# Key norms of an l2-normalised attention: spread over the key columns through DRAM, or transposed on TensorE and read by the exponentials as scales

## The chip, the core and the metric

The kernel runs on one core of one Trainium2 chip. A core has five engines, each with its own in-order instruction queue: TensorE (PE in the profile; its weight loads are listed as PEld), VectorE (DVE), ScalarE (ACT), GpSimd (POOL) and SyncE (SP, which here only starts DMAs). They work on a scratchpad of 128 partitions (SBUF) and on eight accumulator banks (PSUM, 2 KB per partition each), and wait for each other through semaphores.

The metric is the device time of one execution in microseconds (us), lower is better. Before the change three runs took 1624.97, 1627.02 and 1626.72 us, median 1626.72. The profile comes from one further execution.

## The reference, cut to what matters

The input is 8 sequences (batches) of 512 rows of 256 numbers. A layer of attention with 16 heads of 64 and a feed-forward part of four layers of width 1024 follow each other, each between two layer norms and with a residual.

```python
q = (x @ w_q).reshape(b, s, h, -1).transpose(0, 2, 1, 3)
...
q = _l2norm(q) * jnp.exp(scale)      # t / max(norm(t), 1e-12), per row and head
k = _l2norm(k)
sim = jnp.einsum('bhid,bhjd->bhij', q, k)
attn = jax.nn.softmax(sim, axis=-1)
out = jnp.einsum('bhij,bhjd->bhid', attn, v)
out = out.transpose(0, 2, 1, 3).reshape(b, s, h * out.shape[-1])
return out @ w_out + b_out
```

A score is the product of a query and a key, divided by the norm of each. The division by the key's norm can stand before the product, on the key, or behind it, on the score: it is one factor per key and head.

## The kernel before

**Where things lie.** The attention is computed transposed. For a batch and a half of the heads (8 heads, `hf` is 0 or 1) `qT` and `kT` hold four tiles of 128 x 512: the partitions are the 64 dimensions of two heads, the columns the 512 positions. A unit is a batch and a pair of heads (64 units). `scores` multiplies, for one block `jb` of 128 key positions, each head's keys with its queries: the result `s` has the 128 keys on the partitions and 2 x 512 columns, one bank for each head. One exponential over all 1024 columns (L555) gives `e`, without the subtraction of a maximum, since scores are bounded. `values` multiplies `e` with the values into `po`; `summed` adds the four blocks' `e` on DVE, and `row_sums` sums over the keys on PE for the softmax's denominator.

**The norms before.** `norms_step(b, hf, which)` runs for `which` "q" and "k". The squares (L427) are summed over each head's dimensions by four matmuls with a constant of ones and zeros (`pn`, L456), which leave each head's 512 sums on 16 equal partitions. ACT copies them to SBUF (`nd`, L480). A DMA takes one row of each head and folds the 8 x 512 numbers into 128 x 32 (`nf`, L462), DVE puts a floor under them (L488), POOL raises them to the power -1/2 (L312). For queries only, DVE multiplies by the head's exponentiated scale (L495). A DMA stores them to DRAM (L502), two more read them back, each head's row repeated over its 64 partitions (`spread`, L470), and four multiplications on DVE (L512) bring `qT` or `kT` to unit length. So a norm's way goes PE, ACT, DMA, DVE, POOL, DMA, DMA, DVE, and the scores of the half wait at its end.

**What sets the order.** All work of the attention is handed to `Steps`: each step names its engine, an estimated length, what it reads, writes and which rotating buffers it takes. PE's steps keep the order in which they are added; the other engines' steps are sorted by a small simulation in which of those that are ready the one with the earliest due time goes first. The order so found is fixed in the program. A loop over the units adds the scores of the next unit, the values of the present one, and from a `plan` by slots (two slots a unit, 16 a batch) the projections, norms, output projections and layer norms of neighbouring batches. In the first batch all projections come ahead of the units. In later ones the first half of a batch is prepared in the second part of the batch before it (keys' norm products at slot 9, values at 9 and 11 to 13), the second half in the batch's own first slots (norm products at slot 2, values at 3, 5, 6 and 7, among the previous batch's output projections at 2 to 5). DVE and SP have a second task in the first 300 us: all feed-forward weights are loaded (L854), looked through (L861, L866), combined and stored (L898, L902).

**Buffers that matter here.** The pool `ps_w` has three PSUM buffers, taken in turn by all projections, norm products, row transposes and row sums; a taker waits until the buffer of the third before it has been read. `ps_s` has two buffers of two banks for `s`, so the scores of a block wait for the exponential two blocks earlier. `sqp` has two SBUF buffers, for `nd` and the copied row sums. `ep` has six for `e`, `spreadp` two for the squares and the spread norms.

Of the kernel before, what the change touches and what calls it, by code (L numbers as in the profile page):

```python
# [12 lines left out]
AF = mybir.ActivationFunctionType  # L13
ALU = mybir.AluOpType
# [3 lines left out]
P = 128  # L18
LN_EPS = 1e-5
NORM_FLOOR = 1e-12  # L20
# [119 lines left out]
def tile_fast(  # L140
# [41 lines left out]
    nc = tc.nc  # L182

    B, S, D = x.shape
# [4 lines left out]
    NT = S // P  # L189
# [5 lines left out]
    HH = H // 2  # L195
# [4 lines left out]
    small = ctx.enter_context(tc.tile_pool(name="small", bufs=4))  # L200
# [8 lines left out]
    ident = const.tile([P, P], F32, name="ident")  # L209
# [16 lines left out]
    xres, T = {}, {}  # L226
# [14 lines left out]
    escale = const.tile([P, 2], F32, name="escale")  # L241
# [31 lines left out]
    for name, src in (("s1", s1), ("s2", s2), ("hs1", hs1), ("hs2", hs2)):  # L273
        t = const.tile([P, NH], F32, tag=name, name=f"{name}_sb")
# [7 lines left out]
    ep = attn_scope.enter_context(tc.tile_pool(name="ep", bufs=6))  # L282
# [4 lines left out]
    ps_w = attn_scope.enter_context(tc.tile_pool(name="ps_w", bufs=3, space=PSUM))  # L287
# [4 lines left out]
    steps = Steps()  # L292
# [6 lines left out]
    def bounded():  # L299

        nc.vector.tensor_reduce(top, escale, AX.X, ALU.max)
        nc.vector.tensor_scalar(over, top, SCORE_BOUND, None, ALU.is_gt)
        nc.vector.tensor_scalar_min(escale, escale, SCORE_BOUND)
# [3 lines left out]
        writes=[("escale", 0)], earliest=landed["escale"],  # L307
# [3 lines left out]
    def power(d, n):  # L311
        nc.gpsimd.tensor_tensor(d, d, neghalf.to_broadcast([P, n]), ALU.pow)  # L312

    def tile_of(pool, shape, tag, key, dtype=F32, bufs=None):
        T[key] = pool.tile(shape, dtype, tag=tag, bufs=bufs, name="_".join(str(k) for k in key))
        return T[key]
# [127 lines left out]

    def norms_step(b, hf, which):

        n = (which, b, hf)
        pn, d, f, r = ("pn", *n), ("nd", *n), ("nf", *n), ("spread", *n)
        to = (which + "T", b, hf)
        r_dram = dram.tile([HH, S], F32, tag=f"n{which}_{b}_{hf}", name=f"n{which}_{b}_{hf}")  # L450
        NF = HH * S // P

        def products():
            tile_of(ps_w, [P, S], "w", pn)
            for j in range(HP):
                nc.tensor.matmul(  # L456
                    T[pn][ts(j, 32), :], lhsT=halves_of, rhs=T[r][:, j, :], start=True, stop=True
                )

        def folded():  # L460
            tile_of(small, [P, NF], "nf", f, bufs=2)
            nc.sync.dma_start(  # L462
                T[f],
                T[d][::16, :].rearrange("i (c n) -> i c n", c=16),
            )

        def spread():
            tile_of(spreadp, [P, HP, S], "spread", r)
            for h in range(2):
                nc.sync.dma_start(  # L470
                    T[r][ts(h, DH)],
                    r_dram.rearrange("(j h) s -> h j s", h=2)[h : h + 1].to_broadcast([DH, HP, S]),
                )

        steps.add(
            "pe", 0.86, products, reads=[(r, j) for j in range(HP)], writes=[(pn, 0)],
            takes=[("w", 3, pn)], tiling=("col", 32),
        )
        steps.add(
            "act", 0.59, lambda: nc.scalar.copy(tile_of(sqp, [P, S], "sq", d), T[pn]),  # L480
            reads=[(pn, 0)], writes=[(d, 0)], takes=[("sq", 2, d)],
        )
        steps.add(
            "sync", 0.1, folded, reads=[(d, 0)], writes=[(f, 0)], takes=[("nf", 2, f)], lag=1.8
        )
        steps.add(
            "dve", 0.12,
            lambda: nc.vector.tensor_scalar_max(T[f], T[f], NORM_FLOOR * NORM_FLOOR),  # L488
            writes=[(f, 0)],
        )  # L490
        steps.add("pool", 6.0, lambda: power(T[f], NF), writes=[(f, 0)])
        if which == "q":
            steps.add(
                "dve", 0.12,
                lambda: nc.vector.tensor_scalar(  # L495
                    T[f], T[f], escale[:, hf : hf + 1], None, ALU.mult
                ),
                reads=[("escale", 0)], writes=[(f, 0)],
            )
        steps.add(  # L500
            "sync", 0.1,
            lambda: nc.sync.dma_start(r_dram.rearrange("i (c n) -> (i c) n", c=16), T[f]),  # L502
            reads=[(f, 0)], writes=[(("rd", *n), 0)], lag=1.5,
        )
        steps.add(
            "sync", 0.2, spread, reads=[(("rd", *n), 0)], writes=[(r, j) for j in range(HP)],
            lag=7.5,
        )
        for j in range(HP):
            steps.add(  # L510
                "dve", 0.69,
                lambda j=j: nc.vector.tensor_tensor(  # L512
                    T[to][:, j, :], T[to][:, j, :], T[r][:, j, :], ALU.mult
                ),
                reads=[(r, j)], writes=[(to, j)],
            )

    def v_step(b, hf, t):
        pm, to = ("vp", b, hf, t), ("v", b, hf)
        projected(pm, b, t, wkv_sb, INNER + hf * HALF)  # L520

        def copied():
            if t == 0:
                tile_of(vp, [P, NT, HALF], "v", to)
            nc.scalar.copy(T[to][:, t, :], T[pm])

        steps.add(
            "act", 0.59, copied, reads=[(pm, 0)], writes=[(to, t)],
            takes=[("v", 2, to)] if t == 0 else (),
        )  # L530

    def scores(b, p, jb):

        hf, j = divmod(p, HP)
        qT, kT, s, e = ("qT", b, hf), ("kT", b, hf), ("s", b, p, jb), ("e", b, p, jb)

        def products():
            tile_of(ps_s, [P, 2, S], "s", s)
            for h in range(2):
                hp = slice(h * DH, (h + 1) * DH)  # L540
                nc.tensor.matmul(  # L541
                    T[s][:, h, :],
                    lhsT=T[kT][hp, j, ts(jb, P)],
                    rhs=T[qT][hp, j, :],
                    start=True,
                    stop=True,
                )

        steps.add(
            "pe", 0.86, products, reads=[(kT, j), (qT, j)],  # L550
            writes=[(s, 0)], takes=[("s", 2, s)], tiling="row",
        )
        steps.add(
            "act", 1.03,
            lambda: nc.scalar.activation(tile_of(ep, [P, 2, S], "e", e), T[s], AF.Exp),  # L555
            reads=[(s, 0)], writes=[(e, 0)], takes=[("e", 6, e)],
        )

    def summed(b, p, jb):
# [208 lines left out]
    def at(slot, step):  # L768
        plan.setdefault(slot, []).append(step)
# [11 lines left out]
    def v_plan(b, hf, slots):  # L781
        for t, s in enumerate(slots):
            at(s, lambda t=t: v_step(b, hf, t))

    def next_rows(b, slot, some):
        if b < B:
            for t in some:
                at(slot + t // 2, lambda t=t: norm_in(b, "a", t, ("xres", b)))

    for b in range(B):  # L790
        base = b * NSLOT
        next_rows(b + 1, base, (0, 2))
        if b:
            qk_plan(b, 1, [base + s for s in (-2, -2, -1, -1, 0, 0, 1, 1)], (base, base + 2))
        next_rows(b + 1, base, (1, 3))
        if b:
            v_plan(b, 1, [base + s for s in (3, 5, 6, 7)])
            for t in range(NT):
                at(base + 2 + t, lambda b=b, t=t: out_proj(b - 1, t))
            n = b - 1 + NX  # L800
            if n < B:
                at(base + 6, lambda n=n: loads(n))
            elif n < B + 2:
                at(base + 6, lambda c=n - B: reloads(c))
        if b + 1 < B:
            qk_plan(
                b + 1, 0, [base + s for s in (6, 6, 7, 7, 8, 8, 9, 9)], (base + 8, base + 9),
                lambda b=b: v_step(b + 1, 0, 0),
            )
            for t in range(1, NT):  # L810
                at(base + 10 + t, lambda b=b, t=t: v_step(b + 1, 0, t))

    def loads(b):
        steps.add(
            "sync", 0.1, lambda: load_x(b), lag=4.0, writes=[(("xres", b), t) for t in range(NT)],
            takes=[("xres", NX, ("xres", b))],
        )
# [128 lines left out]
    for t in range(NT):  # L946
        v_step(0, 0, t)
        if t == 0:
            norms_step(0, 0, "k")
    for w in "qk":  # L950
        for j in range(HP):
            qk_step(0, 1, w, j)
    norms_step(0, 1, "q")
    for t in range(NT):
        v_step(0, 1, t)
    norms_step(0, 1, "k")
    units = [(b, p) for b in range(B) for p in range(NP)]
    for g in range(2):
        for jb in (2 * g, 2 * g + 1):
# [1 line left out]
    for k, u in enumerate(units):  # L961
# [3 lines left out]
        for g in range(2):  # L965
# [3 lines left out]
            if g == 0:  # L969
# [5 lines left out]
                b, p = u  # L975
# [16 lines left out]
    for t in range(NT):  # L992
# [6 lines left out]
        reads=[(("e", *units[-1], NT - 1), 0)],  # L999
# [36 lines left out]
    before, steps = steps, Steps()  # L1036
# [966 lines left out]
```

## Time and profile before

| | us |
|---|---|
| Median of three runs | 1626.72 |
| The profiled execution, whole | 1627.83 |
| Its span, first to last instruction | 1626.0 |
| Attention, up to the feed-forward part's first matmul | about 1022 |
| Steady batch (start of its first scores to that of the next, 397.60 to 523.05) | 125.4 |
| PE, DVE, ACT, POOL busy in 300 to 426 | 125.8, 57.3, 65.3, 27.2 |

The page shows busy time by engine, the busy share of 40 equal slices of the span, DMA queues, the chain of work that ended last, and groups of instructions: line, engine, operation, output and inputs, shapes, count, then busy time, mean ns of one, and the engine's idle time before them with what ended it. The timeline lists instructions in order of time with start and length, equal ones merged; in brackets stands the idle time before them and its releaser. The clock column is TensorE's granted clock as a share of full speed.

```profile
PE   9999999999999999999999999999999999999997
DVE  3587886454354363363363375869786987879686
ACT  4665445545545535635535634466566646654663
POOL 4211303302212122122112120447155426534451
PEclk9999999999999999999999999999999999999999
DMA  6446555222133122122122131444414532452440
```

PE's row is at nine tenths or more from end to end. The groups of the key chain that are on DVE, POOL and ACT:

```profile
L512 DVE TENSOR_TENSOR kT<-kT,spread_k 128x512 f32<-128x512 f32 x64 | 41.7, 685 | 18.3 <-DMA spread_k<-nk 13.2 <-ACT spread_k L427 5.1
...
L480 ACT COPY nd_k<-pn_k 128x512 f32<-128x512 f32 x16 | 9.4, 585 | 4.4 <-PE pn_k L456 3.9 <-DVE mv_a L332 0.5
...
L488 DVE TENSOR_SCALAR nf_k<-nf_k 128x32 f32<-128x32 f32 x16 | 2.8, 178 | 22.1 <-DMA nf_k<-nd_k 22.1
```

### The profile page before, as it was taken

The page shows a single profiled execution, that of the slowest core. Times are in us where ns is not written, and L with a number is a line of the kernel's source. Part 1 is how long each engine was busy: PE and PEld are TensorE (multiplying, and loading weights), DVE is VectorE, ACT ScalarE, POOL GpSimd, SP SyncE. Part 2 cuts the span into 40 slices and gives each one's busy share as a digit, 9 for nine tenths or more (in the row PEclk, how much of TensorE's full clock was granted, in tenths as well). Part 3 has the DMA queues.
Part 4 walks back from the last instruction along what each step waited for, and adds up shares of the span by engine and source line. Part 5 has one row for each costly group of instructions (what it writes and reads, how often), then busy time and mean ns, then how long its engine had stood idle before and what let it go on. Part 6 is the DMA issues. An engine that isn't in the chain of part 4 may idle for free.

```text
span 1626.0 us, 18855 instructions
## 1 busy us (share of the span) xinstructions
PE 1603.5 (99%) x6808; PEld 915.9 (56%) x6808; DVE 1023.9 (63%) x1708; ACT 878.2 (54%) x1343; POOL 487.5 (30%) x356
## 2 busy tenths in 40 slices
PE   9999999999999999999999999999999999999997
PEld 4333443443443443353353354788888888888886
DVE  3587886454354363363363375869786987879686
ACT  4665445545545535635535634466566646654663
POOL 4211303302212122122112120447155426534451
PEclk9999999999999999999999999999999999999999
DMA  6446555222133122122122131444414532452440
GB/s 177 119 139 169 151 181 132 68 66 67 41 79 67 42 79 67 41 74 63 43 75 66 29 92 27 143 129 132 147 61 143 156 113 79 141 157 66 132 154 29
DMA packets 91042, 159.91 MB, mean 98 GB/s; under 512 B 23868, under 2 KB 39484, under 8 KB 86844
## 3 DMA queue, kind: packets, MB, share of 16 engines
q1 hardware_dynamic: 71324, 95.71, 22.3%
q0 software_dynamic: 18912, 61.87, 12.3%
q8 instruction: 55, 0.90, 0.2%
q10 hardware_dynamic: 704, 1.05, 0.2%
q14 instruction: 47, 0.39, 0.1%
HBM read 140.26 MB, written 17.56 MB: 97 GB/s over the span
## 4 chain that ended last, share of the span: by engine, by line
PE 82%; DVE 3%; issue 2%; DMA 2%; POOL 1%; ACT 1%; SPq 0%; DVEq 0%; POOLq 0%
PE g L1256 25%; PE s L541 12%; PE po L586 11%; PE p L1182 6%; PE pa L711 6%; PE kp L411 5%; PE qp L411 5%; PE vp L387 5%; PE py L1370 3%; PE pd L609 2%; DMA spread_k<-nk 1%; POOL nf_k L312 1%; DMA nk<-nf_k 1%; PE pn_q L456 1%; PE pn_k L456 1%
## 5 line engine op out<-in xcount | busy, mean ns | idle before, releaser
L555 ACT ACTIVATE e<-s 128x1024 f32<-128x1024 f32 x256 | 248.2, 1021 | 120.8 <-PE s L541 120.3
L541 PE MATMUL s<-qT,kT 64*128 64x512 f32 x1024 | 255.8, 618 | 6.2 <-DVE kT L512 4.7
L586 PE MATMUL po<-e,v 128*64 128x512 f32 x1024 | 234.4, 600 | 0.0
L1256 PE MATMUL g<-h,wb_S 128*128 128x512 f32 x1024 | 234.3, 389 | 0.0
L312 POOL TENSOR_TENSOR nf_q<-nf_q,neghalf 128x32 f32<-128x32 f32 x16 | 88.0, 5499 | 439.2 <-DVE nf_q L488 439.2
L1256 PEld LDWEIGHTS g<-h,wb_S 128*128 128x128 f32 x1024 | 192.0, 188 | 39.8
L566 DVE TENSOR_TENSOR es<-es,e 128x1024 f32<-128x1024 f32 x128 | 156.6, 1224 | 87.9 <-ACT e L555 83.0
L541 PEld LDWEIGHTS s<-qT,kT 64*128 64x128 f32 x1024 | 88.0, 186 | 159.7 <-issue 115.0
L1256 PE MATMUL g<-h,wb_A 128*128 128x512 f32 x768 | 176.4, 389 | 0.0
L1256 PEld LDWEIGHTS g<-h,wb_A 128*128 128x128 f32 x768 | 144.0, 188 | 29.8
L586 PEld LDWEIGHTS po<-e,v 128*64 128x64 f32 x1024 | 68.0, 137 | 159.3 <-issue 158.8
L566 DVE TENSOR_TENSOR es<-e,e 128x1024 f32<-128x1024 f32 x64 | 78.3, 1223 | 119.3 <-PE pd L609 98.5
L1074 DVE TENSOR_TENSOR h<-C,h 128x512 fp32r<-128x512 f32 x112 | 129.4, 1211 | 3.9 <-ACT h L1064 3.8
L1074 DVE TENSOR_TENSOR h<-B,h 128x512 fp32r<-128x512 f32 x112 | 107.9, 1003 | 26.9 <-ACT h L1064 26.7
L312 POOL TENSOR_TENSOR nf_k<-nf_k,neghalf 128x32 f32<-128x32 f32 x16 | 89.0, 5562 | 117.1 <-issue 96.6
L387 PE MATMUL vp<-wkv_sb,aT 128*128 128x512 f32 x256 | 120.6, 602 | 0.0
L711 PE MATMUL pa<-wo_sb,oT 128*128 128x256 f32 x512 | 117.2, 382 | 0.0
L411 PE MATMUL kp<-aT,wkv_sb 128*128 128x512 f32 x256 | 115.8, 601 | 1.4 <-ACT kT L422 1.4
L1312 POOL TENSOR_TENSOR B<-B,B 128x512 f32<-128x512 f32 x64 | 102.0, 1621 | 43.7 <-DVE B L1213 38.8
L411 PE MATMUL qp<-aT,wq_sb 128*128 128x512 f32 (+1 forms) x272 | 114.3, 570 | 0.0
L711 PEld LDWEIGHTS pa<-wo_sb,oT 128*128 128x128 f32 x512 | 95.9, 190 | 31.1 <-issue 17.5
L681 ACT COPY oT<-po 128x512 f32<-128x512 f32 x64 | 37.5, 586 | 140.5 <-PE po L586 140.5
(131 smaller groups left out, 2079.2 us busy)
## 6 DMA issues: line engine op xcount, KB each, us to landing
wb_S<-s POOLq DMA_DIRECT2D x32, 1024.0 KB, 5.1
spread_q<-nq SPq DMA_DIRECT2D x32, 512.0 KB
spread_k<-nk SPq DMA_DIRECT2D x32, 512.0 KB
rden<-r SPq DMA_DIRECT2D x62, 256.0 KB
wb_A<-in_h1T_dram POOLq DMA_DIRECT2D x12, 1024.0 KB, 5.5
wb_A<-in_h2T_dram POOLq DMA_DIRECT2D x12, 1024.0 KB, 5.6
s<-w SPq DMA_DIRECT2D x32, 256.0 KB
w<-in_h1T_dram SPq DMA_DIRECT2D x8, 512.0 KB
```

The lines of the kernel that those rows point to most:

```text
L312: nc.gpsimd.tensor_tensor(d, d, neghalf.to_broadcast([P, n]), ALU.pow)
L387: nc.tensor.matmul(pm, lhsT=T["aT", b][:, c, ts(t, P)], rhs=w[:, c, c0 : c0 + HALF], start=(c == 0), stop=(c == ND - 1),)
L411: nc.tensor.matmul(T[pm][:, cols], lhsT=w[:, c, c0 : c0 + P], rhs=T["aT", b][:, c, cols], start=(c == 0), stop=(c == ND - 1),)
L541: nc.tensor.matmul(T[s][:, h, :], lhsT=T[kT][hp, j, ts(jb, P)], rhs=T[qT][hp, j, :], start=True, stop=True,)
L555: lambda: nc.scalar.activation(tile_of(ep, [P, 2, S], "e", e), T[s], AF.Exp),
L566: nc.vector.tensor_tensor(T[t], T["e", b, p, 0] if jb == 1 else T[t], T["e", b, p, jb], ALU.add)
L586: nc.tensor.matmul(T[po][h * DH : (h + 1) * DH, :], lhsT=T[v][:, jb, c0 : c0 + DH], rhs=T[e][:, h, :], start=(jb == 0), stop=(jb == NT - 1),)
L711: nc.tensor.matmul(banks(), lhsT=T["oT", b, p][:, ts(t, P)], rhs=wo_sb[:, p, :], start=(p == 0), stop=(p == NP - 1),)
L1074: lambda: nc.vector.tensor_tensor(T[h][:, 1, c, :], T[raw][:, c, :], T[h][:, 0, c, :], ALU.subtract),
L1182: nc.tensor.matmul(T[ps[k]], lhsT=(w1r, w2r)[k][c][:, ts(o, P)], rhs=row_halves(b, i)[0][:, c, :], start=(c == 0 and i == 0), stop=(c == N ...
L1256: nc.tensor.matmul(T[to[o]], lhsT=T[w][:, c, ts(o, P)], rhs=T[h][:, i, c, :], start=(first and c == 0 and i == 0), stop=(c == NQ - 1 and i ...
L1312: lambda: (nc.gpsimd if T_ENGINE == "pool" else nc.vector).tensor_tensor(T[dst][:, c, :], T[x][:, c, :], T[y][:, c, :], ALU.subtract),
```

## The change

For keys, `norms_step` ends with the copy `nd`. A new `key_norms` transposes that copy in four blocks of 128 positions, so that a key's position is on the partition, and takes every sixteenth column, one for each head: `kn` is 128 x 4 x 8, a reciprocal norm for every key position (128 x 4 blocks) and head (8). `kT` stays as projected. The exponential multiplies its input by a scale per partition, the key's reciprocal norm; since that differs between the two heads of a unit, one exponential of 1024 columns becomes two of 512. Queries go the old way.

```diff
@@ norms_step
             reads=[(pn, 0)], writes=[(d, 0)], takes=[("sq", 2, d)],
         )
+        if which == "k":
+            return
         steps.add(
             "sync", 0.1, folded, reads=[(d, 0)], writes=[(f, 0)], takes=[("nf", 2, f)], lag=1.8
         )
...
+    def key_norms(b, hf):
+        d, pk, kn = ("nd", "k", b, hf), ("pk", b, hf), ("kn", b, hf)
+        def transposes():
+            tile_of(ps_w, [P, NT, P], "w", pk)
+            for jb in range(NT):
+                nc.tensor.transpose(T[pk][:, jb, :], T[d][:, ts(jb, P)], ident)
+        def bounded():
+            tile_of(small, [P, NT, HH], "kn", kn, bufs=3)
+            nc.vector.tensor_scalar_max(T[kn], T[pk][:, :, ::16], NORM_FLOOR * NORM_FLOOR)
+        steps.add(
+            "pe", 0.44, transposes, reads=[(d, 0)], writes=[(pk, 0)], takes=[("w", 3, pk)],
+            tiling="full",
+        )
+        steps.add("dve", 0.15, bounded, reads=[(pk, 0)], writes=[(kn, 0)], takes=[("kn", 3, kn)])
+        steps.add(
+            "pool", 5.7, lambda: power(T[kn].rearrange("p t h -> p (t h)"), NT * HH),
+            writes=[(kn, 0)],
+        )
@@ scores
-        steps.add(
-            "act", 1.03,
-            lambda: nc.scalar.activation(tile_of(ep, [P, 2, S], "e", e), T[s], AF.Exp),
-            reads=[(s, 0)], writes=[(e, 0)], takes=[("e", 6, e)],
-        )
+        def exponentials():
+            tile_of(ep, [P, 2, S], "e", e)
+            for h in range(2):
+                nc.scalar.activation(
+                    T[e][:, h, :], T[s][:, h, :], AF.Exp,
+                    scale=T["kn", b, hf][:, jb, 2 * j + h : 2 * j + h + 1],
+                )
+        steps.add(
+            "act", 1.2, exponentials,
+            reads=[(s, 0), (("kn", b, hf), 0)], writes=[(e, 0)], takes=[("e", 6, e)],
+        )
```

The order of PE's steps is kept, with the transposes put in: for a second half at slot 3, behind the values' block 0 and the second output projection that go before it, for a first half at slot 11, behind the values' block 1. In the first batch they stand behind the values' block 2, and the second half's key norm products move from behind all four blocks of values to behind the first.

```diff
+            at(base + 3, lambda b=b: key_norms(b, 1))
...
+                if t == 1:
+                    at(base + 10 + t, lambda b=b: key_norms(b + 1, 0))
...
     for t in range(NT):
         v_step(0, 1, t)
-    norms_step(0, 1, "k")
+        if t == 0:
+            norms_step(0, 1, "k")
+        if t == 2:
+            key_norms(0, 1)
```

More of the change, by code (lines that the diff above doesn't have):

```diff
@@ L491, in norms_step @@
         steps.add("pool", 6.0, lambda: power(T[f], NF), writes=[(f, 0)])
-        if which == "q":
-            steps.add(
[L494 to L498, printed above, removed]
-            )
+        steps.add(
+            "dve", 0.12,
+            lambda: nc.vector.tensor_scalar(
+                T[f], T[f], escale[:, hf : hf + 1], None, ALU.mult
+            ),
+            reads=[("escale", 0)], writes=[(f, 0)],
+        )
         steps.add(
@@ L949, in tile_fast @@
             norms_step(0, 0, "k")
+        if t == 2:
+            key_norms(0, 0)
     for w in "qk":
@@ L955, in tile_fast @@
         v_step(0, 1, t)
-    norms_step(0, 1, "k")
+        if t == 0:
+            norms_step(0, 1, "k")
+        if t == 2:
+            key_norms(0, 1)
     units = [(b, p) for b in range(B) for p in range(NP)]
```

## The prediction

> **What bounds the kernel now.** I read the page's busy shares first, then stretches of the span, then the waits of TensorE (PE) with their places.
>
> ```profile
> PE 1603.5 (99%) x6808; PEld 915.9 (56%) x6808; DVE 1023.9 (63%) x1708; ACT 878.2 (54%) x1343; POOL 487.5 (30%) x356
> ...
> 140.00:150.00 10.00, 7.96 (x33) 2.35 (x32) 5.05 (x8) 3.09 (x4) 0.00 (x0) 0.83 0.56 156
> ...
> 300.00:426.00 126.00, 125.76 (x493) 51.70 (x491) 57.31 (x98) 65.32 (x93) 27.18 (x13) 1.00 0.25 60
> 426.00:552.00 126.00, 125.52 (x490) 51.68 (x490) 57.33 (x98) 65.48 (x95) 27.12 (x13) 1.00 0.26 61
> ```
>
> PE is busy 1603.5 of 1626.0 us. The two long windows are one batch each in the middle of attention (start, width, then busy time of PE, weight loads, DVE, ACT, POOL, then clock, DMA share, GB/s): PE idles 0.2 to 0.5 us of 126, ACT and DVE work half the time. There, whatever is added to PE's queue is added to the time, and whatever is taken from ACT, DVE, SP or the DMA queues is worth nothing. The key chain that the change removes can pay only where PE waits for it. The waits on L512 (the multiplication by the spread norms) and PE's timeline say where that is:
>
> ```profile
>   PE s L541: 4.7, 3
> ...
> 142.27 3.07 PE L541 MATMUL s<-qT,kT 64*128 64x512 f32 x8 [2.04 <-DVE kT L512]
> 145.27 4.21 PE L586 MATMUL po<-e,v 128*64 128x512 f32 x16
> ...
> 212.19 1.99 PE L541 MATMUL s<-qT,kT 64*128 64x512 f32 x8 [1.25 <-DVE kT L512]
> ...
> 272.16 1.99 PE L541 MATMUL s<-qT,kT 64*128 64x512 f32 x8 [1.41 <-DVE kT L512]
> ```
>
> Three waits, 4.7 us in all, while weight checks crowd DVE and SP; from 300 us on there is none. After the first, the window 140 to 150 shows a granted clock of 0.83, and eight score matmuls take 3.07 where they otherwise take 1.99, sixteen value matmuls 4.21 instead of 3.65: 1.08 + 0.56 = 1.64 us more.
>
> **Removed, per key half (16 of them).** One fold DMA, one store, two spreads on SP's queue, and four DVE multiplications (L512, 64 of 0.685 us, 41.7 us with their overlap). None is on PE. Gain: the three waits, 4.7, and the slowed clock behind the first, 1.64. The scores then wait for queries only, whose last multiplication ended at 135.6 for the scores of 142.3. Bounds: 4.7 if the clock dips anyway; 6.5 with a 0.20 us wait of pn_q at 45.6, which goes because the changed start squares the queries earlier. I take 6.5.
>
> [...] The trace has the dip behind a gap of 2.04 us and none behind 1.25 and 1.41. [...]
>
> **Added on PE.** Four transposes per key half, 64 in all. The rows transposes have the same form:
>
> ```profile
> 425.40 0.60 PE L344 MATMUL pt_a<-ident,xn_a 128*128 128x128 f32 x4
> ...
> L344 PE MATMUL pt_a<-ident,xn_a 128*128 128x128 f32 x64 | 11.5, 282 | 0.8 <-ACT aT L349 0.6
> ```
>
> Four take 0.60 with one's length of about 0.27 at the end, so (0.60 - 0.27) / 3 = 0.11 from start to start, 0.44 for four, and 16 x 0.44 = 7.0 us. In the changed instruction order each four follow a value or output projection, which use the whole array as they do, so no change of array layout comes with them, save one more at the start (about 0.1, dropped). Bounds: 7.0, and 64 x 0.282 = 18.0 if none overlaps its neighbour; the first is the nearer row. All of it is on the path. They wait for ACT's copy nd_k, made over 6 us ahead (118.96 against some 129 in the first such place), and for one of the three rotating PSUM buffers; the tightest is the second half's, where the buffer of the first output projection must have been read: DVE does that at most 2.8 us after its end, and 5.3 us of PE work lie between.
>
> **Added on ACT.** 256 exponentials of 1024 columns become 512 of 512 columns with a scale read per partition. The trace has no such exponential; the FFN's activations with a scale from PSUM are nearest.
>
> ```profile
> 76.15 1.94 ACT L555 ACTIVATE e<-s 128x1024 f32<-128x1024 f32 x2 [0.43 <-PE s L541]
> ...
> 1053.82 1.28 ACT L1203 ACTIVATE sg<-p,s_sb 128x512 f32<-128x512 f32 x2
> ...
> L555 ACT ACTIVATE e<-s 128x1024 f32<-128x1024 f32 x256 | 248.2, 1021 | 120.8 <-PE s L541 120.3 <-DVE y L861 0.3 <-ACT e L555 0.2
> L1203 ACT ACTIVATE sg<-p,s_sb 128x512 f32<-128x512 f32 x64 | 44.0, 689 | 75.3 <-PE p L1182 58.9 <-DVE B L1213 16.2
> L1293 ACT COPY C<-g 128x512 f32<-128x512 f32 x96 | 54.8, 589 | 42.7 <-PE g L1256 42.7
> L1281 ACT ACTIVATE C<-C,hs_sb 128x512 f32<-128x512 f32 x96 | 68.6, 723 | 47.6 <-DVE C L1303 47.5
> ```
>
> Two scaled activations take 1.28, each 0.69, so 0.59 from start to start. The exponentials of two score blocks, now 1.94, become four halves: 3 x 0.59 + 0.69 = 2.46, that is 0.52 more. Bounds: no price for the scale (the copies, 0.59 long, 0.10 of it overlapped as between the Silus: 3 x 0.49 + 0.59 = 2.06, 0.12 more); the row that reads SBUF (0.723, overlapping as much: 3 x 0.62 + 0.72 = 2.58, 0.64 more). I take 0.52. In the steady batches this is hidden. I set each score matmul beside the end of the exponential that last read its buffer: 1.6 us lie between at the tightest steady place, 1.4 us between exponential and value matmul at the very end, over 3.5 us elsewhere. ACT in order delays copies behind an exponential too, but the copies that PE waits for (0.24 each at the third key projection of seven batches) start after ACT's own idle of 0.47, so they don't move. The cover is gone where score blocks follow each other without values between:
>
> ```profile
> 77.23 2.04 PE L541 MATMUL s<-qT,kT 64*128 64x512 f32 x8 [0.27 <-ACT e L555]
> ```
>
> That is at 77, 85, 985 and 993 us (four blocks in a row) and 57 to 59 (six). The fourth block now waits for the second exponential: 0.52 less the 0.05 that was free, 0.47, four times 1.9. The sixth waits for four exponentials: seven starts of 0.59 and one length, 4.82, against 4.19 now (55.78 to 59.97), 0.6. One row transpose at 68.1 waits for a copy behind exponentials: 0.5. Sum 3.0 (bounds about 0.7 and 3.7).
>
> **Moved.** The max (0.18 us on DVE) now reads PSUM, and the power on POOL (5.4 to 5.8 us, as before) has a new waiter: the first exponential of a half, and behind it all of ACT, then PE after two score buffers. In a steady first half the transposes would end near 386.9, the max is done by 388.6 (DVE has the first query multiplication and one sum of 1.22 ahead), the power by 394.1; that exponential would start near 399, after scores at 397.6 now. In second halves some 16 us of PE work lie between. I cost it at nothing; the cover is 5 us. SP's queue only gets shorter: no DMA is added or moved ahead of another.
>
> **Sum.** 7.0 + 3.0 - 6.5 = +3.5 us, so the span goes from 1626.0 to 1629.5. The profiled run took 1627.83, 1.1 above the median of 1626.72; the step is applied to the median: 1630.2. About 0.2%, 3.3 us, is what a measurement can tell from no change, so the forecast lies just on the slower side of it.
>
> **Rivals.**
> - *The scale is free on ACT* (not slower). Place: the five runs of adjacent score blocks. Four halves in 2.06 instead of 2.46 leave a growth of 0.7 instead of 3.0: 7.0 + 0.7 - 6.5 = +1.2, 1627.9. It decides from some 2.4 us for four halves downward, where the sum falls below 3.3. For: copies of that shape take 0.589. Against: both scaled groups take 0.69 and 0.72.
> - *The scales come late.* ACT stands before the first exponential of a half. It decides when max and power end more than 5 us later than worked out, as when DVE's max sits behind a query multiplication whose spread lands late (waits up to 4.2 us are in the trace). At 3 us each in seven first halves: 1651.
> - *ACT becomes the bound in the steady batches.* Needs pairs 1.6 us longer, halves near 0.95 from start to start. At 0.2 us over that, some seven tight places in each of seven batches: 7 x 7 x 0.2 = 10, 1640. Against: ACT would stay near 60% busy by the rows.
> - *Transposes at full length.* 18.0 instead of 7.0: 1641. Against: the row of four.
>
> **How the numbers follow.** Forecast 0.60 (1628.5 to 1632), free scale 0.18, late scales 0.08, ACT bound 0.08, long transposes 0.06. The forecast alone straddles the bound: 0.35 slower, 0.24 same, 0.01 faster. The free scale gives 0.13 same and 0.05 faster, since with it a wait or two more gone would reach -3.3. The last three are slower, 0.22. Together faster 0.06, same 0.37, slower 0.57. The range runs from 1625, below the free scale by the worth of one wait, to 1640, which takes in most of the ACT bound and leaves out the late scales.
>
> **What would show it.** Right: no wait of the scores on DVE; pk transposes 0.11 us apart; exponentials of 0.69; waits of about 0.5 to 0.8 us at the adjacent score blocks and nowhere else; a middle batch 0.9 us longer than 125.4. Wrong: exponentials waiting on POOL; s waiting on ACT in the middle batches; a granted clock below 1.00 near 142 us though nothing waits there.

## The result and the profile after

Eight runs of the changed kernel took 1631.07 to 1634.24 us, median 1632.4; eight of the kernel before, beside them, 1624.97 to 1630.03, median 1627.45. The ratio is 1.0029 (95% interval 1.0018 to 1.0040): 5 us slower, 0.3%. The profiled execution took 1633.7 with a span of 1631.9. The page's busy shares, the first DMA queue and the chain that ended last:

```profile
PE 1610.9 (99%) x6872; PEld 924.2 (57%) x6872; DVE 988.5 (61%) x1644; ACT 938.1 (57%) x1599; POOL 491.7 (30%) x356
...
q1 hardware_dynamic: 58140, 78.40, 17.3%
...
PE 96%; DVE 1%; ACT 1%; DMA 0%; issue 0%; POOL 0%; ACTq 0%; POOLq 0%
```

PE has 64 instructions more, the transposes, and 7.4 us more of busy time. DVE lost 64 multiplications and 35 us, ACT gained 256 exponentials and 60 us, and the first DMA queue moves 17 MB less (78.4 for 95.7). The chain that ended last is now PE for 96% of the span, 82% before.

PE's stretch at 142 us and one steady window (the columns are those of the windows shown of before: start, width, busy time of PE, weight loads, DVE, ACT, POOL, clock, DMA share, GB/s), then PE's timeline of the first:

```profile
140.00:150.00 10.00, 10.00 (x40) 3.42 (x36) 9.63 (x14) 6.03 (x11) 0.51 (x1) 1.00 0.69 211
...
426.00:552.00 126.00, 125.87 (x496) 52.37 (x496) 52.70 (x90) 72.12 (x125) 26.71 (x13) 1.00 0.18 43
```

```profile
144.86 1.99 PE L567 MATMUL s<-qT,kT 64*128 64x512 f32 x8
146.78 3.65 PE L619 MATMUL po<-e,v 128*64 128x512 f32 x16
```

The wait of 2.04 and the clock of 0.83 are gone: eight score matmuls take 1.99 again and sixteen value matmuls 3.65. In the steady batches DVE gave up 4.6 us and the DMA share fell from 0.26 to 0.18, worth nothing, while ACT has 72.1 us of 126. From the first scores of one batch to those of the next it is now 126.32 (397.49 to 523.81), 0.87 more than before.

PE's waits in the whole span (engine and line, what it waited for, us in total, times, longest):

```profile
PE s L567 <- ACT e L582: 3.1, 6, 0.9
...
PE pt_a L344 <- ACT aT L349: 1.1, 1, 1.1
...
PE qp L411 <- DVE kn L532: 0.8, 1, 0.8
```

No score matmul waits for DVE any longer. The six waits on exponentials are the adjacent score blocks, which had waits already and have longer ones now. The last line is new.

The account of the two profiled executions, up to the first matmul of the feed-forward part (1021.86 before, 1026.64 after):

| | us |
|---|---|
| 64 transposes, 16 x 0.44 | +7.0 |
| four places with four adjacent score blocks, 0.48 each | +1.9 |
| the place with six, 6.49 to 7.59 from first scores to first values | +1.1 |
| row transpose at 71 us, wait 0.64 to 1.12 | +0.5 |
| new wait of a query projection at 34 us | +0.75 |
| three waits of scores on spread keys | -4.7 |
| clock behind the first of them | -1.64 |
| wait of pn_q (0.20) gone, first 8 us shorter by 0.09 | -0.3 |
| sum | +4.6 |
| measured | +4.8 |

From there to the end the execution after took 605.27 us, the one before 604.19: 1.1 us more, with a stretch of lower clock at the start of the feed-forward part (3.4 us at 0.50) that has nothing to do with the edit (shown below).

### The profile page after: what moved, and what is told of

Read it like the earlier page. It is cut to its first block, busy times and chain, and to the rows that moved or that the text cites. A ratio compares the mean times of both kernels' runs of the same rounds, so it can differ in the third digit from the quotient of the medians.

```text
span 1631.9 us, 19063 instructions
## 1 busy us (share of the span) xinstructions
PE 1610.9 (99%) x6872; PEld 924.2 (57%) x6872; DVE 988.5 (61%) x1644; ACT 938.1 (57%) x1599; POOL 491.7 (30%) x356
## 4 chain that ended last, share of the span: by engine, by line
PE 96%; DVE 1%; ACT 1%; DMA 0%; issue 0%; POOL 0%; ACTq 0%; POOLq 0%
PE g L1297 25%; PE s L567 15%; PE po L619 14%; PE pa L744 7%; PE kp L411 7%; PE qp L411 7%; PE p L1223 7%; PE vp L387 7%; PE py L1411 4%; PE pd L642 2%; PE pn_q L458 1%; PE pn_k L458 1%; ACT e L582 1%; PE pk L528 0%; PE ptf L1167 0%
## 5 line engine op out<-in xcount | busy, mean ns | idle before, releaser
L582 ACT ACTIVATE e<-s,kn 128x512 f32<-128x512 f32 x512 | 309.5, 687 | 117.8 <-PE s L567 117.3
L599 DVE TENSOR_TENSOR es<-e,e 128x1024 f32<-128x1024 f32 x64 | 78.4, 1225 | 174.0 <-PE pd L642 141.5
L312 POOL TENSOR_TENSOR kn<-kn,neghalf 128x32 f32<-128x32 f32 x16 | 93.1, 5818 | 91.3 <-DVE kn L532 79.5
L1353 POOL TENSOR_TENSOR C<-C,C 128x512 f32<-128x512 f32 x64 | 94.1, 1496 | 27.7 <-DVE h L1115 27.2
```

Source lines behind the costliest of these rows:

```text
L582: nc.scalar.activation(T[e][:, h, :], T[s][:, h, :], AF.Exp, scale=T["kn", b, hf][:, jb, 2 * j + h : 2 * j + h + 1],)
L599: nc.vector.tensor_tensor(T[t], T["e", b, p, 0] if jb == 1 else T[t], T["e", b, p, jb], ALU.add)
L1353: lambda: (nc.gpsimd if T_ENGINE == "pool" else nc.vector).tensor_tensor(T[dst][:, c, :], T[x][:, c, :], T[y][:, c, :], ALU.subtract),
```

## The experiments

### The exponentials whole again, the transposes kept

```diff
         def exponentials():
-            tile_of(ep, [P, 2, S], "e", e)
-            for h in range(2):
-                nc.scalar.activation(T[e][:, h, :], T[s][:, h, :], AF.Exp,
-                    scale=T["kn", b, hf][:, jb, 2 * j + h : 2 * j + h + 1])
+            nc.scalar.activation(tile_of(ep, [P, 2, S], "e", e), T[s], AF.Exp)
```

> The changed kernel with its exponentials whole again (one of 1024 columns, no scale), transposes, max and power kept: the key norms are computed and not used, so the division by them is left out. Theory (the transposes lengthen the steady batch, the split exponentials cost only where score blocks stand side by side): a middle batch stays at 126.3 us from first scores to first scores, the waits of the adjacent score blocks are 0.27 again with pairs of 2.04, and the time is 3 to 3.5 us below the changed kernel, about 1629, ratio to before 1.001. Rival (longer exponentials lengthen the steady batch): a middle batch of 125.4 us and about 1622, ratio 0.997.

Measured: 1628.15 us (1627.88 to 1630.04), ratio to before 1.0011 (0.9999 to 1.0024), span 1626.0. The kernel before, timed beside this run and the next three, had a median of 1626.30, beside the changed kernel 1627.45. So there are two ways to set a run against the changed kernel: this one lies 4.2 us below it by the medians, 2.9 by the ratios. Its exponentials, and the second pair of blocks at one four-block place:

```profile
L580 ACT ACTIVATE e<-s 128x1024 f32<-128x1024 f32 x256 | 248.1, 1021 | 120.9 <-PE s L567 120.9
...
78.00 2.05 PE L567 MATMUL s<-qT,kT 64*128 64x512 f32 x8 [0.27 <-ACT e L580]
```

The same place in the changed kernel:

```profile
80.78 2.28 PE L567 MATMUL s<-qT,kT 64*128 64x512 f32 x8 [0.51 <-ACT e L582]
```

A wait longer by 0.24 and a pair longer by 0.23, because the fourth block stands for the last half of the second exponential: 0.47 to 0.48 a place. With whole exponentials all these waits are those of before again (0.27 and 0.21, the row transpose 0.64), and the steady batch keeps the changed kernel's 126.32. So the splitting costs only where score blocks are adjacent, and the steady growth is not its.

### The scales without the transposes

```diff
-            nc.vector.tensor_scalar_max(T[kn], T[pk][:, :, ::16], NORM_FLOOR * NORM_FLOOR)
+            nc.vector.tensor_scalar_max(
+                T[kn], T[d][:, ::16].rearrange("p (t h) -> p t h", t=NT), NORM_FLOOR * NORM_FLOOR)
-        steps.add("pe", 0.44, transposes, ...)
```

> The changed kernel without the 64 transposes and without their PSUM buffer: the floor reads the copied sums as they lie, so each exponential gets a scale that is not its key's. Theory: a middle batch of 125.4 us (0.87 less), the wait of 0.75 us at 34 us gone, the split exponentials' waits kept; 7.0 + 0.75 = 7.8 us below the changed kernel, about 1624.7, ratio to before 0.998. Rival (the exponentials lengthen the batch): a middle batch stays at 126.3 and the time near 1632.

Measured: 1625.79 us (1625.08 to 1626.92), ratio 0.9995 (0.9981 to 1.0008), 6.6 below the changed kernel by the medians, 5.5 by the ratios; steady batch 125.44 (393.31 to 518.75), with the waits of 0.51, 0.89 and 1.12 of the split exponentials all there. The whole 0.87 per batch is the transposes. The 7.8 expected was too much: 0.75 of it was the wait at 34 us, which the later profiles of the changed kernel do not have.

### Scales only for the three halves whose scores waited

The kernel before, with the new way for the keys of batch 1, both halves, and batch 2, first half.

```diff
+AS_SCALES = {(1, 0), (1, 1), (2, 0)}
...
+        if which == "k" and (b, hf) in AS_SCALES:
+            return
...
+    def key_norms(b, hf):
+        if (b, hf) not in AS_SCALES:
+            return
...
+            if (b, hf) not in AS_SCALES:
+                nc.scalar.activation(T[e], T[s], AF.Exp)
+                return
```

> A version that may beat both: the kernel before, with transposes and scales only in the three halves whose scores waited for the keys (batch 1 both halves, batch 2 first half). Theory: the three waits (4.7 us) and, if the dip of the clock belongs to the first, 1.6 us more go; three times 0.44 us of transposes come, no adjacent score blocks lie in these halves: 1627.45 - 4.7 - 1.6 + 1.3 = 1622.4, ratio 0.997; without the clock's part 1624.0, ratio 0.998. Rival (the waits are replaced by waits for queries or for POOL's power in the same places): no faster than before, 1627 to 1629, with s waiting on DVE or ACT near 142, 212 or 272 us.

Measured: 1622.79 us (1621.85 to 1624.72), ratio 0.9977 (0.9966 to 0.9988): by the medians 3.5 us faster than before and 9.6 faster than the full change (8.5 by the ratios). PE at the first of the three places, and the group of split exponentials:

```profile
137.15 3.70 PE L388 MATMUL vp<-wkv_sb,aT 128*128 128x512 f32 x8
140.78 1.99 PE L571 MATMUL s<-qT,kT 64*128 64x512 f32 x8
```

```profile
L589 ACT ACTIVATE e<-s,kn 128x512 f32<-128x512 f32 x96 | 58.1, 688 | 24.9 <-PE s L571 24.9
```

No brackets, so no wait. 48 of 256 exponentials are split (96 halves), none of them at adjacent blocks, and 12 transposes replace three waits. Steady batches go back to 125.44. The gain here is the removed waits (and whatever clock they cost) less 12 x 0.11 = 1.3 us; with 3.5 measured, the waits were worth 4.8, between 3.3 and 6.8 by the ratio's interval. That is too wide to tell whether the clock's 1.6 us belongs to it.

### Halves without a scale

The kernel before, each exponential in two of 512 columns and no scale.

```diff
-            lambda: nc.scalar.activation(tile_of(ep, [P, 2, S], "e", e), T[s], AF.Exp),
+            lambda: (tile_of(ep, [P, 2, S], "e", e),
+                [nc.scalar.activation(T[e][:, h, :], T[s][:, h, :], AF.Exp) for h in range(2)]),
```

> The kernel before with each exponential in two halves of 512 columns and no scale; all else as before. Theory (a scale read per partition costs about 0.1 us an instruction, a half without it costs as a copy): halves 0.59 long, 0.48 from start to start, four in about 2.05; waits of the adjacent score blocks about 0.1 us longer than 0.27; time 0.5 to 1 us above before, ratio 1.0004. Rival (splitting itself costs what the changed kernel shows): halves 0.69 long, 0.57 from start to start, and 2.5 to 3 us above before, ratio 1.0017.

Measured: 1627.73 us (1625.39 to 1633.37), ratio 1.0012 (0.9997 to 1.0027). The group here, and that of the changed kernel:

```profile
L557 ACT ACTIVATE e<-s 128x512 f32<-128x512 f32 x512 | 264.0, 602 | 115.6 <-PE s L541 115.5
```

```profile
L582 ACT ACTIVATE e<-s,kn 128x512 f32<-128x512 f32 x512 | 309.5, 687 | 117.8 <-PE s L567 117.3
```

The scale costs 85 ns of length. From start to start two neighbouring halves are 0.477 us apart without it and 0.570 with it, so 93 ns there. Four halves take 2.03 without a scale and 2.40 with it, where whole exponentials take 1.94; the adjacent places grow by 0.13 instead of 0.48. Most of the price of the split is the scale operand, not the second instruction. The time alone would not decide it: its interval takes in both expected ratios, 1.0004 and 1.0017.

This run brought a surprise: the key chain is the old one, yet its waits are not the 2.04, 1.25 and 1.41 of before.

```profile
141.94 1.99 PE L541 MATMUL s<-qT,kT 64*128 64x512 f32 x8 [0.30 <-DVE kT L512]
...
209.67 1.99 PE L541 MATMUL s<-qT,kT 64*128 64x512 f32 x8 [0.70 <-DVE kT L512]
...
268.94 1.99 PE L541 MATMUL s<-qT,kT 64*128 64x512 f32 x8 [0.72 <-DVE kT L512]
```

So the next question was how much of the expected gain belonged to one execution.

### The kernel before, profiled twice more

> The kernel before, unchanged, profiled a second time. Theory (the waits of the scores for the multiplied keys depend on when the spread DMAs land, which differs from one execution to the next): the three waits, 2.04, 1.25 and 1.41 us in the first profile, have other lengths, their sum differs by 1 us or more, and where none is near 2 us the granted clock near 142 us stays at 1.00. Rival (the waits belong to the program's order): the same three waits within 0.2 us, with the same dip of the clock behind the first.

> The kernel before, unchanged, profiled a third time. As for the second: by the theory, waits of other lengths and a span that differs with their sum; by the rival, the first profile again.

The first took 1623.92 us (span 1622.1), the second 1625.77 (span 1624.0). The score matmuls that waited, first execution:

```profile
141.60 1.99 PE L541 MATMUL s<-qT,kT 64*128 64x512 f32 x8 [1.69 <-DVE kT L512]
...
209.16 1.99 PE L541 MATMUL s<-qT,kT 64*128 64x512 f32 x8 [0.53 <-DVE kT L512]
...
268.14 1.99 PE L541 MATMUL s<-qT,kT 64*128 64x512 f32 x8 [0.42 <-DVE kT L512]
```

and second:

```profile
141.68 1.99 PE L541 MATMUL s<-qT,kT 64*128 64x512 f32 x8 [1.81 <-DVE kT L512]
...
209.79 1.99 PE L541 MATMUL s<-qT,kT 64*128 64x512 f32 x8 [1.08 <-DVE kT L512]
...
269.43 1.99 PE L541 MATMUL s<-qT,kT 64*128 64x512 f32 x8 [1.08 <-DVE kT L512]
```

The same program at the same three places: 4.70 us in all in the first profile, 2.64 and 3.97 in these. The length behind the first wait is 1.99 in both, not 3.07: no lower clock follows, though 1.69 and 1.81 are near the 2.04 that had one. The spans go with the waits: up to the feed-forward part's first matmul the three took 1021.86, 1017.83 and 1019.12 us. The third is 1.29 above the second, with waits 1.33 longer; the first is 4.03 above it, with waits 2.06 longer and 1.64 of lower clock.

### The changed kernel again, and with its power done twice

> The changed kernel, unchanged, profiled a second time. Theory: from the first scores of batch 1 on the attention takes the same time to 0.1 us (no wait in it hangs on a DMA), what differs lies in the first 60 us, where the query norms still go through DMAs, and in dips of the granted clock, such as the 0.91 behind the waits of 0.99 and 0.56 us at the start of the feed-forward part, which by the other traces comes only now and then. Rival (the changed kernel has a dip of its own there): the dip again, and a span of 1631.5 to 1632.5.

1631.65 us, span 1629.8. Six batches agree with the first profile to a hundredth: 757.90 us from the first scores of batch 1 to those of batch 7 in both (144.86 to 902.76 and 143.81 to 901.71). The waits of 0.51, 0.89 and 1.12 are there; the wait of 0.75 at 34 us and the lower clock at the feed-forward part's start are not.

The second kernel raises each key half's sums to the power 1 on POOL behind the power -1/2.

```diff
+        steps.add(
+            "pool", 5.7,
+            lambda: nc.gpsimd.tensor_tensor(
+                T[kn].rearrange("p t h -> p (t h)"), T[kn].rearrange("p t h -> p (t h)"),
+                ones[:, :1].to_broadcast([P, NT * HH]), ALU.pow),
+            writes=[(kn, 0)],
+        )
```

> The changed kernel with a second power (exponent 1, same shape) on POOL behind each key half's first, 5.4 to 6.3 us more before the scales are ready. Theory (the power lies behind 5.6 us of cover in first halves, 10.4 us and more in the others): second halves lose nothing, each of the seven later first halves at most about 0.7 us, so 0 to 5 us over the changed kernel. Rival (the scales are on the path already): 16 times 5.4, some 86 us more.

1630.9 us, span 1629.1, steady batch 126.32. The added group, and ACT's waits for it:

```profile
L545 POOL TENSOR_TENSOR kn<-kn,ones 128x32 f32<-128x32 f32 x16 | 87.7, 5482 | 1.3
```

```profile
ACT e L590 <- POOL kn L545: 4.3, 7, 0.6
```

88 us more on POOL moved nothing on PE. In the seven later first halves the idle time of some 0.6 us before the first exponential is now put down to POOL, where it was 0.57 for the scores: in batch 3 the second power ends at 397.44, and the exponential starts 1.31 us behind its first scores instead of 1.26. So doubling the power has just used up the cover.

## Why the prediction was right, and where it was not

**The bound** was right. What was added to PE's queue came out in full (0.87 us a batch) and what was taken from DVE, SP and the DMAs was worth nothing wherever PE did not wait (4.6 us of DVE in a steady batch, which grew by those 0.87).

**The transposes**, 7.0, were right to the digit: 0.87 a batch measured against 0.88, the four 0.60 long as in the row of the row transposes. The price of about 0.1 that the prediction gives a change of array layout has a counterpart in the profile of before: query projections start at 412.13 and 412.56, 0.43 apart, and the scores behind them, in another layout, at 413.08, 0.52 later, while a key projection at 424.97 and the transpose behind it, in one layout, are 0.43 apart. This is the timeline ahead of the first half of batch 3, from its transposes to its first exponential on all engines:

```profile
385.91 0.60 PE L528 MATMUL pk<-ident,nd_k 128*128 128x128 f32 x4
...
386.55 0.19 DVE L532 TENSOR_SCALAR kn<-pk 128x32 f32<-128x32 f32 x1
386.89 6.27 POOL L312 TENSOR_TENSOR kn<-kn,neghalf 128x32 f32<-128x32 f32 x1 [12.19 <-DVE kn L532]
...
397.49 1.99 PE L567 MATMUL s<-qT,kT 64*128 64x512 f32 x8
...
398.75 1.84 ACT L582 ACTIVATE e<-s,kn 128x512 f32<-128x512 f32 x3 [0.57 <-PE s L567]
```

**The moved power** was rightly costed at nothing. It ends at 393.16, 5.6 us before the exponential that reads it; the prediction had 5. The max was 2 us earlier than worked out, the power nearly a microsecond longer. The doubled power shows the cover from the other side.

**The adjacent score blocks** were the right mechanism and, at the four places, the right size: 1.9 predicted and measured. The two terms behind it, 0.59 from start to start and 0.69 long, measured 0.57 and 0.687. Two small errors cancel in the 1.9: four halves came to 2.40, not 2.46, and the 0.05 taken off as free was not free, since the pair of 2.04 before, 1.99 elsewhere, shows the fourth block waiting already. The row transpose's 0.5 was right too. The copies that PE waits for did not move, as predicted; those waits of 0.24 are six, not seven. The place with six blocks was mis-sized: 0.6 predicted, 1.1 measured. PE and ACT there, after:

```profile
56.34 1.99 PE L567 MATMUL s<-qT,kT 64*128 64x512 f32 x8
59.22 2.28 PE L567 MATMUL s<-qT,kT 64*128 64x512 f32 x8 [0.89 <-ACT e L582]
61.72 2.29 PE L567 MATMUL s<-qT,kT 64*128 64x512 f32 x8 [0.21 <-ACT e L582]
63.93 3.65 PE L619 MATMUL po<-e,v 128*64 128x512 f32 x16
```

```profile
57.90 7.41 ACT L582 ACTIVATE e<-s,kn 128x512 f32<-128x512 f32 x12 [0.87 <-PE s L567]
```

The first exponential starts 1.56 us after its scores; before it was 1.18 (54.60 to 55.78). Those 0.38 and 0.12 more for the twelve halves than worked out make the missing 0.5. The exponential has two things to wait for now, PE and POOL, but the second wait does not explain the 0.38. In both profiles of the change the first exponentials of the other 15 halves have the same two and start 1.23 to 1.26 after their scores (397.49 to 398.75 above), at most 0.08 later than before. The first exponential of all is late (1.55 or 1.56) in all four executions profiled in which it has a scale, and is not (1.18) with whole exponentials or halves without a scale. In the hybrid, where scales begin in batch 1, the first scaled one starts after 1.26. Why the delay comes only there stays open.

**The gain of 6.5** is the term that failed in size: three waits and a lower clock, read from one execution, were priced as the kernel's own. In the pair of profiled executions it came in full: waits and lower clock are both gone. But it was that execution's, not the kernel's: the three waits came to 4.70, 2.64 and 3.97 in three executions of the same program, and the clock's 1.64 came in one of them only. By the medians, the added terms as measured, 7.0 and 3.5, less the difference of 4.95 leave a gain of 5.5, and the hybrid gives 4.8; with their intervals about 3 to 7.5. The forecast of +3.5 took the upper end. What makes up the 2.2 us between the forecast of 1630.2 and the median of 1632.4: 0.7 is the kernel before itself, whose median in the eight runs is 1627.45; 0.5 the place with six blocks; 1.0 the gain.

Why the waits differ follows from what hangs on them: they end with a multiplication behind three DMAs in a row (fold, store, read back) that run while the weights are loaded. The traces show it. At the first of the three places, from ACT's copy of the sums (L480) to DVE's first multiplication (L512):

| | copy starts | multiplication starts | us between | wait of the scores |
|---|---|---|---|---|
| before, first profile | 118.96 | 141.43 | 22.47 | 2.04 |
| before, second | 118.65 | 140.76 | 22.11 | 1.69 |
| before, third | 118.61 | 140.84 | 22.23 | 1.81 |
| halves without a scale | 120.39 | 141.11 | 20.72 | 0.30 |

The wait is each time what the chain takes beyond 20.42 or 20.43 us. POOL's power in it is 5.77 or 5.78 long in all four; what varies lies with the DMAs. SP issues the two spreads 3.89 to 5.26 us after the store, and the multiplication, which waits for them, starts 7.71 to 9.25 us after that.

The times of the runs fit that. The kernel before ranges over 10 us (1622.97 to 1633.12 in 35 runs) and the halves without a scale, with the same chain, over 8 (10 runs); the kernels in which no scores wait for it range over 1.8 (no transposes, 10 runs), 2.2 (whole exponentials, 10), 2.9 (hybrid, 12) and 3.2 (the change, 8). A part of those 10 us goes with the clock: of the 35 runs three had a mean granted clock of 0.995, with times up to 1633.12. But the 15 runs at 0.998 still lie 5.2 apart (1622.97 to 1628.14). That this rest is the chain's, in executions that were not profiled, was not shown.

**A wait that was not foreseen** cost 0.75 us in the first profile of the change. DVE and PE there:

```profile
31.80 0.24 DVE L498 TENSOR_SCALAR nf_q<-nf_q,escale 128x32 f32<-128x32 f32 x1 [2.59 <-POOL nf_q L312]
32.32 1.96 DVE L337 TENSOR_SCALAR xn_a<-xres,mv_a,rs_a 128x256 f32<-128x256 f32 x4 [0.27 <-POOL rs_a L312]
34.20 0.18 DVE L532 TENSOR_SCALAR kn<-pk 128x32 f32<-128x32 f32 x1
```

```profile
29.65 0.60 PE L528 MATMUL pk<-ident,nd_k 128*128 128x128 f32 x4
...
34.44 5.42 PE L411 MATMUL qp<-aT,wq_sb 128*128 128x512 f32 x12 [0.75 <-DVE kn L532]
```

The transposes hold one of the three rotating buffers until DVE's max has read it. In batch 0 that max stood behind the queries' own scaling, which was 2.59 us late, and four normalisations of rows; the third taker after the transposes, a query projection, had to wait. The prediction looked at the buffer that the transposes take and never at the one they hold. With whole exponentials that scaling began at 28.58 instead of 31.80 and there was no such wait; in the two later profiles with transposes and split exponentials there was none either, so of the three executions with both one had it.

**The rivals.** The scale is not free (85 ns of length, 93 from start to start). The scales are never late by a microsecond, even with the power doubled (0.6 at most). ACT is no bound at 72 us of 126, and no score matmul waits for it in the middle batches. Transposes do overlap their neighbours (four take 0.60 us, one 0.273).

**The clock.** The prediction went by the row that had a lower clock behind 2.04 us. Gaps of 1.69 and 1.81 at the same place had none, and in the feed-forward part one came behind gaps of 0.99 and 0.56. PE in the kernel before, third profile:

```profile
1030.35 0.50 PE L1182 MATMUL p<-fT,wr 128*128 128x512 f32 x1 [0.99 <-DVE B L1213]
...
1032.11 0.50 PE L1182 MATMUL p<-fT,wr 128*128 128x512 f32 x1 [0.56 <-ACT sg L1203]
1032.44 0.43 PE L1182 MATMUL p<-fL,wr 128*128 128x512 f32 x1
1032.67 0.62 PE L1182 MATMUL p<-fT,wr 128*128 128x512 f32 x1
```

The matmuls go from 0.39 to about 0.62 for 3.4 us. The window 1010 to 1050 of this execution and of the second profile of before:

```profile
1010.00:1050.00 40.00, 37.94 (x166) 30.66 (x167) 31.73 (x69) 16.32 (x29) 13.48 (x17) 0.96 0.47 146
```

```profile
1010.00:1050.00 40.00, 37.69 (x171) 30.26 (x170) 33.25 (x72) 17.23 (x31) 15.48 (x19) 1.00 0.48 145
```

Gaps of 0.99 and 0.56 stand there in all ten profiles of this study; the clock fell in two of them, here and in the first profile of the change. It is a matter of the execution, and a second execution is what tells it from an effect of an edit.

The three drops are alike in length and depth. In the first profile of before the window 143.03 to 146.45 shows a clock of 0.50, and the 3.4 us on either side of it 1.00. In the change the window 1039.88 to 1043.29 shows 0.50 and its neighbours of the same width 1.00. Here, where the window 1022 to 1041 shows 0.91, the matmuls of 0.59 to 0.63 stand between 1032.67 and 1036.08; in the change they were 0.61 to 0.63. The length of a gap does not tell which one has a drop behind it: 0.99 and 0.56 had one in two executions and none in eight, and 2.04 had one where 1.69 and 1.81 had none. What sets those apart stays open.

## What to carry to other kernels

On a kernel whose TensorE is never idle (99% busy here), a step moved onto it costs its full length at every place, while it pays only where TensorE waited: here 16 places paid 0.44 us and three had waits, and doing it at those three alone beat both kernels. A wait that ends with a DMA should be read from several executions before its removal is priced (4.70, 2.64 and 3.97 us here). Split an instruction only where its reader does not stand directly behind it (0.47 to 0.48 us a place here), and ask of every rotating buffer not only when it is free to take but who must read it before the next can have it (0.75 us in one execution here).

## What the hardware showed beyond that

- A scale read from a 128 x 1 operand lengthened an exponential of 512 columns from 0.602 to 0.687 us and widened the distance between two from 0.477 to 0.570. That is 85 ns of length and 93 from start to start.
- Where the program's very first exponential had a scale from memory, it started 1.55 or 1.56 us after its scores, 0.38 later than without one; in the changed kernel the first of every other half was at most 0.08 later. The cause is open.
- The granted clock fell behind gaps of 0.99 and 0.56 us in two executions of ten, behind one of 2.04, and not behind gaps of 1.69 and 1.81. Each drop lasted 3.4 us, at a clock of 0.50 in the two whose windows show it. The cause is open.
